# Core products of a triangle layer: two of three channels with one half-width product less, plain channels row block by row block, squares in PSUM banks that are tiles of their own

## The chip, the core and the metric

The kernel runs on one core of one Trainium2 chip. The metric is the device time of one execution in microseconds (us), as the median of several runs. A core has these engines: TensorE for matrix products (PE in the profile, with its weight loads as PEld), VectorE (DVE), ScalarE (ACT), GpSimd (POOL) and SyncE (SP), which here issues nearly all DMAs. Each engine works through its own queue in order, and semaphores make one wait for another. TensorE writes its results into PSUM, eight banks of 512 float32 numbers per partition; VectorE and ScalarE read and write PSUM and SBUF[...].

## The reference, cut to what matters

Two layers act on x of shape 1 x 384 x 384 x 128, in float32. The part that the change touches is the einsum of the first layer and the layer norm over channels that follows it.

```python
z = layernorm(x)
left  = (z @ Wl + bl) * sigmoid(z @ Wlg + blg)        # [i, k, h]
right = (z @ Wr + br) * sigmoid(z @ Wrg + brg)        # [j, k, h]
core  = einsum('bikh,bjkh->bijh', left, right)        # 128 channels h, each a 384x384x384 product
zo = layernorm(core, over h) @ Wout + bout
x1 = x + sigmoid(x @ Wg + bg) * zo
# second layer, row by row: left' = x1 @ (Wleft + Weq), right' summed over the row,
# out = (left' * rowsum * sigmoid(x1 @ Wgate)) @ Wout1;  result = layernorm(out + x1)
```

For one channel h the core is a product of two 384 x 384 matrices, that is of 3 x 3 blocks of 128 on the left side against 384 columns on the right. The layer norm over h needs, for each (i, j), the sum and the sum of squares of the core over all channels.

## The kernel before, in words

There are three stages. Stage 1 (to about 1012 us) normalises x, computes left and right and stores them to DRAM in `lr_d`, channel by channel; the last two row groups are kept in SBUF (`kept`). Stage 2 (about 1012 to 1737 us) computes the core, one channel after the other, and stores it to `core_d`. Stage 3 does the rest, row by row. Nearly every instruction goes through `seq`, so each engine's queue has the order in which the Python code issues it.

Stage 2, in which the change lies, has a loop over the channels h = 0 to 125; the last two, 126 and 127, follow in other code. With `NB = 3`, `N = 384`, `P = 128` and `J = 192`:

- `load_h` (L92) loads a channel's left and right parts, interleaved, from `lr_d` into a tile `lrh`, in two DMAs: 384 KB (the block k = 0) and 640 KB (k = 1 and most of k = 2). There are three such tiles. Each pass of the loop issues the load of h + 3 at its end, when channel h's tile is free.
- `stay` (L610, POOL) copies the kept rows of channel h + 1 into its tile, in block k = 2. `fill` (L585 to L592, POOL) does the like and the cast for the channels 0 and 127.
- `apart` (L632, ACT) casts the right part, which is interleaved in `lrh`, to a contiguous tile `rr`, one block k at a time; k = 0 needs the first DMA, k = 1 the second, k = 2 that and `stay`.
- A plain channel (before: even h) takes nine full-width products (128 x 128 against 384 columns), into one PSUM tile `pc` of three banks, for k outer and row block i inner. ACT copies the tile to SBUF as `ct` (L689) one channel later.
- A split channel (before: odd h) saves products by a scheme with sums of blocks in the manner of Strassen and Winograd: three full-width products for row block 2 (into bank `b4`), and eleven products of half width (192 columns) for the row blocks 0 and 1, into the banks `b0` to `b3`. Of the left side it needs four sums `ss` (`left_sums`, L618, POOL), of the right side four sums `tt` (`right_sums2`, L623 to L628, POOL); these are prepared one channel ahead, in the order stay, left sums, right sums. VectorE adds the partial results (`add`, L651): four adds to form terms, and four to write `ct`. ACT copies `b0` (L692) and `b4` (L696).
- `store_core` (L645, SP) stores `ct` (576 KB). `add_sum` (L638, VectorE) adds a channel to `csum`; `squares` (L635, ACT) squares `ct` into SBUF (`sq`), and `add_squares` (L642, VectorE) adds that to `csq`. Each is one instruction of 1152 columns.

Two engines that read the same PSUM tile do so one after the other, in program order. The three banks of `pc` are one tile; `b0` to `b4` are one each. SBUF sums and terms lie in one tile, `arena`, of eight rows of 384 columns.

Of the kernel before, what the change touches and what calls it, by code (L numbers as in the profile page):

```python
# [8 lines left out]
F32 = mybir.dt.float32  # L9
AF = mybir.ActivationFunctionType  # L10
# [4 lines left out]
P = 128  # L15
# [4 lines left out]
def triangle_then_gated_row_kernel(ctx: ExitStack, tc: tile.TileContext, a: dict, out: bass.AP):  # L20
# [13 lines left out]
    nc = tc.nc  # L34
    x_nat, x_tok, x_row = a["x_nat"], a["x_tok"], a["x_row"]
    NG8, C = x_nat.shape[1], x_tok.shape[2]
    N = 8 * NG8
    H = a["L0_side_b"].shape[0] // 4
    assert C == P and H == P and N % P == 0
    NB = N // P  # L40
# [15 lines left out]
    def seq(ins):  # L56

        return tc.keep_in_program_order(ins)
# [21 lines left out]
    with ExitStack() as ctx2:  # L80
# [16 lines left out]
        with tc.tile_pool(name="p1w", bufs=5, side="right") as wp, \  # L97
# [47 lines left out]
            wst, g0, b0 = stage[:, 0:4 * H], stage[:, 4 * H:4 * H + 1], stage[:, 4 * H + 1:4 * H + 2]  # L145
            brow, m1, d = stage[:, 5 * H:9 * H], stage[:, 9 * H:10 * H], stage[:, 10 * H:10 * H + 1]
# [16 lines left out]
            wz = const([P, 4 * H], "wz")  # L163
# [281 lines left out]
            for n in range(PLAIN, len(chunks)):  # L445
                k = 2 + (n - PLAIN) // 2
# [74 lines left out]
        arena = spool.tile([P, 2 + 2 * NB, N], F32, name="arena")  # L521
# [39 lines left out]

        with tc.tile_pool(name="p2r", bufs=2, side="right", reuse_waits="tile") as rrp, \
             tc.tile_pool(name="p2more", bufs=1, side="right", reuse_waits="tile") as more, \
             tc.tile_pool(name="p2out", bufs=3, side="right", reuse_waits="tile") as op, \
             tc.tile_pool(name="p2st", bufs=1, side="right", reuse_waits="tile") as stp:
            csum = spool.tile([P, NB, N], F32, name="csum")
            csq = spool.tile([P, NB, N], F32, name="csq")
            seq(nc.vector.memset(csum, 0.0))
# [4 lines left out]
            right = {}  # L573
# [21 lines left out]

            J = N // 2
            js = slice(0, J), slice(J, N)
            one, base, more2, least = (arena[:, n, j] for n in (2, 2 * NB) for j in js)
            tt = arena[:, 0:2].rearrange("p b n -> p (b n)").rearrange("p (q j) -> p q j", j=J)
            ss = [arena[:, 2 * NB + 1, n * P:(n + 1) * P] for n in range(3)] + [stp.tile([P, P], F32, name="s4")]  # L600
            sq = arena[:, NB:2 * NB]
            cts = {}

            def block(h, k, i):
                return loaded2[h][:, k, i * P:(i + 1) * P, 0]
# [5 lines left out]

            def left_sums(h):

                for n, x, y, op in ((0, block(h, 0, 1), block(h, 0, 0), ALU.subtract),
                                    (1, block(h, 0, 1), block(h, 1, 1), ALU.add),
                                    (2, ss[1], block(h, 0, 0), ALU.subtract),
                                    (3, block(h, 1, 0), ss[2], ALU.subtract)):
                    seq(nc.gpsimd.tensor_tensor(ss[n], x, y, op))  # L618

            def right_sums2(h):  # L620

                rr = right[h]
                seq(nc.gpsimd.tensor_tensor(  # L623
                    tt[:, 0:2], rr[:, 0, js[1]].unsqueeze(1).to_broadcast([P, 2, J]),
                    rr.rearrange("p b n -> p (b n)").rearrange("p (a m) -> p a m", a=2)[:, :, js[0]], ALU.subtract,
                ))
                seq(nc.gpsimd.tensor_tensor(tt[:, 2], rr[:, 0, js[0]], tt[:, 1], ALU.subtract))
                seq(nc.gpsimd.tensor_tensor(tt[:, 3], rr[:, 1, js[0]], tt[:, 2], ALU.subtract))  # L628

            def apart(h, k):  # L630

                seq(nc.scalar.copy(right[h][:, k], loaded2[h][:, k, :, 1]))  # L632

            def squares(h):
                seq(nc.scalar.activation(sq, cts[h], AF.Square))  # L635

            def add_sum(h, c=None):
                seq(nc.vector.tensor_add(csum, c or cts[h], csum))  # L638

            def add_squares(h):  # L640
                if h >= 0:
                    seq(nc.vector.tensor_add(csq, csq, sq))  # L642

            def store_core(h, queue=nc.sync):
                seq(queue.dma_start(out=core_d[:, h, :].rearrange("(b p) j -> p b j", p=P), in_=cts[h]))  # L645

            def product(to, lhsT, rhs, start=True, stop=True):
                seq(nc.tensor.matmul(to, lhsT=lhsT, rhs=rhs, start=start, stop=stop))  # L648

            def add(out, ps, term):  # L650
                seq(nc.vector.tensor_add(out, ps, term))  # L651

            def plain(h, banks):

                for k in range(NB):
                    for i in range(NB):
                        product(banks[i], block(h, k, i), right[h][:, k], k == 0, k == NB - 1)

            fill(0)
            with tc.tile_pool(name="p2mix", bufs=1, space=PSUM, reuse_waits="tile") as mps:  # L660
                pc = mps.tile([P, NB, 512], F32, name="pc")
                b0, b1, b2, b3 = (mps.tile([P, 512], F32, name="b%d" % n)[:, :J] for n in range(4))
                b4 = mps.tile([P, 512], F32, name="b4")[:, :N]
                for h in range(H - 2):
                    cts[h] = op.tile([P, NB, N], F32, tag="ct", name="ct")
                    right[h + 1] = rrp.tile([P, NB, N], F32, tag="rr", name="rr")
                    if h % 2 == 0:
                        plain(h, [pc[:, i, :N] for i in range(NB)])
                        if h > 0:
                            store_core(h - 1)  # L670
                        add_squares(h - 2)
                        stay(h + 1)
                        left_sums(h + 1)
                        for k in range(NB - 1):
                            apart(h + 1, k)
                        right_sums2(h + 1)
                        if h > 0:
                            squares(h - 1)
                            add_sum(h - 1)
                        apart(h + 1, NB - 1)  # L680
                        if h > 0:
                            add_squares(h - 1)
                    else:
                        rr, ct = right[h], cts[h]
                        B = [[rr[:, k, j] for j in js] for k in range(NB)]
                        product(b0, block(h, 0, 0), B[0][0])
                        for k in range(NB):
                            product(b4, block(h, k, 2), rr[:, k], k == 0, k == NB - 1)
                        seq(nc.scalar.copy(cts[h - 1], pc[:, :, :N]))  # L689
                        store_core(h - 1)  # L690
                        add_sum(h - 1, pc[:, :, :N])
                        seq(nc.scalar.copy(one, b0))  # L692
                        stay(h + 1)
                        for k in range(NB - 1):
                            apart(h + 1, k)
                        seq(nc.scalar.copy(ct[:, 2], b4))  # L696
                        apart(h + 1, NB - 1)
                        squares(h - 1)
                        product(b1, ss[2], tt[:, 2])
                        product(b2, ss[0], tt[:, 1])  # L700
                        product(b3, ss[1], tt[:, 0])
                        add(base, b1, one)
                        add(more2, b2, base)
                        add(base, b3, base)
                        add(least, b2, base)
                        product(b0, block(h, 1, 0), B[1][0], True, False)
                        product(b0, block(h, 2, 0), B[2][0], False, True)
                        product(b1, ss[3], B[1][1], True, False)
                        product(b1, block(h, 2, 0), B[2][1], False, True)
                        product(b3, block(h, 1, 1), tt[:, 3], True, False)  # L710
                        product(b3, block(h, 2, 1), B[2][0], False, True)
                        product(b2, block(h, 2, 1), B[2][1])
                        add(ct[:, 0, js[0]], b0, one)
                        add(ct[:, 0, js[1]], b1, base)
                        add(ct[:, 1, js[0]], b3, more2)
                        add(ct[:, 1, js[1]], b2, least)
                    del right[h], loaded2[h]
                    load_h(h + 3)
                store_core(h)
            with tc.tile_pool(name="p2ps", bufs=2, space=PSUM, reuse_waits="tile") as ps, \  # L720
                 tc.tile_pool(name="p2one", bufs=1, space=PSUM, reuse_waits="tile") as ps1:
                for h in range(H - 2, H):
# [11 lines left out]
                            start=(kb == 0), stop=(kb == NB - 1),  # L734
                        ))
                    if h == H - 2:
                        add_squares(h - 2)
                        squares(h - 1)
                        add_sum(h - 1)
                        add_squares(h - 1)  # L740
                        fill(h + 1)
                    ct = op.tile([P, NB, N], F32, tag="ct", name="ct")
                    to = core_d[:, h, :].rearrange("(b p) j -> p b j", p=P)
# [362 lines left out]
```

## Time and profile before

| | us |
|---|---|
| median of 3 runs (3136.75 to 3138.16) | 3137.22 |
| profiled execution, its own time | 3139.36 |
| span of the profiled execution | 3137.6 |
| stage 2, first product of channel 0 to first product of channel 126 | 1012.37 to 1725.93 |
| PE busy in the span | 3117.4 |
| DVE busy in the span | 2581.1 |
| POOL busy in the span | 2369.4 |
| ACT busy in the span | 1949.7 |

A row of the profile names the line of the kernel, the engine, the operation, the tile written and the tiles read, the shape, and the count; then the busy time, or in the timeline start and length. In brackets or after a bar stands for how long the engine was idle before and what released it. A float32 product shows as two records (two passes) of PE and of PEld. In the view of waits the columns are the total, the number of times and the longest. POOL's spans are rough.

### The profile page before, as it was taken

Reading aid. Unit: us, or ns where it says so; the run is one execution under the profiler, and the core shown is the slowest. Engines: PE = TensorE matmul, PEld = TensorE weight load, DVE = VectorE, ACT = ScalarE, POOL = GpSimd, SP = SyncE. Lnnn points to the kernel's source line nnn. Section 1 sums busy time; section 2 is a strip of 40 time slices with the busy share of each in tenths; the row PEclk is TensorE's granted clock in tenths of the full one; section 3 lists DMA queues with packets and bytes.
Section 4 is the critical chain, followed back from the end, with each engine's and each line's share of the span. In section 5 each row is a group of like instructions: output and inputs, shape, how many; then the busy total and the mean of one; then the engine's idle time right before and its main releaser. Section 6 shows DMA issues by size and latency. Waiting matters only on the chain.

```text
span 3137.6 us, 47186 instructions
## 1 busy us (share of the span) xinstructions
PE 3117.4 (99%) x11936; PEld 2209.1 (70%) x11936; DVE 2581.1 (82%) x7913; ACT 1949.7 (62%) x4196; POOL 2369.4 (76%) x3003
## 2 busy tenths in 40 slices
PE   9999999999999999999999999999999999999998
PEld 4677777777777777777777666777777777777776
DVE  8888888888886777777776888888888888888998
ACT  4444444444444666656666577777777777777776
POOL 6888888888886565666566588787887887888887
PEclk9999999999999999999999999999999999999999
DMA  4888978788883999999999866666666666666562
GB/s 153 327 312 293 334 276 332 287 321 311 292 333 89 288 289 291 291 290 290 290 290 290 296 213 221 217 222 222 222 222 222 220 223 215 222 218 222 205 216 105
DMA packets 509119, 797.61 MB, mean 254 GB/s; under 512 B 56689, under 2 KB 419569, under 8 KB 492466
## 3 DMA queue, kind: packets, MB, share of 16 engines
q1 hardware_dynamic: 507952, 793.20, 74.5%
q8 instruction: 100, 1.64, 0.2%
q14 instruction: 169, 1.38, 0.1%
q10 hardware_dynamic: 834, 1.18, 0.1%
q0 software_dynamic: 64, 0.20, 0.0%
HBM read 508.14 MB, written 286.36 MB: 253 GB/s over the span
## 4 chain that ended last, share of the span: by engine, by line
PE 98%; DVE 1%; ACT 0%; POOL 0%; issue 0%; DMA 0%; SPq 0%; POOLq 0%; DVEq 0%; ACTq 0%
PE pr L372 31%; PE pc L648 12%; PE b L648 11%; PE py L904 8%; PE pr L875 8%; PE pg L892 8%; PE pl L893 8%; PE pg L844 8%; PE py L905 4%; PE pc L732 0%; DMA stage<-in_x_nat_dram 0%; PE pq L852 0%; PE pt L335 0%; POOL rs L286 0%; DVE lr L385 0%
## 5 line engine op out<-in xcount | busy, mean ns | idle before, releaser
L372 PE MATMUL pr<-wz,xc 128*128 128x512 f32 x2176 | 935.2, 592 | 1.4 <-POOL xc L324 1.4
L372 PEld LDWEIGHTS pr<-wz,xc 128*128 128x128 f32 x2176 | 670.5, 308 | 265.4 <-POOL xc L324 2.7
L383 ACT ACTIVATE sg<-pr,rs 128x256 f32<-128x256 f32 x1152 | 482.8, 470 | 510.8 <-ACT sg L383 355.5
L385 DVE SCALAR_TENSOR_TENSOR lr<-pr,rs,sg 128x256 f32<-128x256 f32 x1152 | 501.9, 477 | 165.6 <-ACT sg L383 160.1
L939 ACT ACTIVATE py<-py,nm,rs 128x128 f32<-128x128 f32 x1149 | 491.9, 429 | 158.5 <-DVE u L897 80.0
L904 PEld LDWEIGHTS py<-wo,u 128*128 128x128 f32 x2304 | 376.6, 191 | 97.5
L904 PE MATMUL py<-wo,u 128*128 128x128 f32 x2304 | 402.0, 275 | 0.0
L866 POOL TENSOR_TENSOR cs<-ct,rt 128x384 f32<-128x384 f32 x380 | 378.7, 998 | 9.5 <-PE pr L875 4.1
L974 POOL TENSOR_TENSOR yt<-yt,lnb 128x384 f32<-128x384 f32 x380 | 379.8, 1001 | 2.9 <-DVE yt L968 2.5
L648 PE MATMUL pc<-rr,lrh 128*128 128x384 f32 x1134 | 376.1, 486 | 0.4 <-DVE lr L385 0.4
L324 POOL TENSOR_TENSOR xc<-xc,bc 128x512 f32<-128x512 f32 x272 | 345.6, 1270 | 24.0
L286 POOL TENSOR_TENSOR rs<-nd,mhalf 128x8 f32<-128x8 f32 (+1 forms) x145 | 236.2, 1629 | 147.0 <-ACT sg L383 107.4
L919 DVE BATCH_NORM_STATS2 st<-py 128x6 f32<-128x128 f32 x1152 | 266.1, 286 | 88.6 <-PE py L905 86.7
L905 PE MATMUL py<-ident,x1T 128*128 128x128 f32 x1152 | 314.0, 273 | 0.0
L875 PE MATMUL pr<-cs,wc 128*128 128x384 f32 x768 | 313.5, 490 | 0.0
L892 PE MATMUL pg<-x1T,mat_L_conv_W_gate 128*128 128x384 f32 x768 | 310.7, 486 | 0.9 <-ACT g L895 0.9
L632 ACT COPY rr<-lrh 128x384 f32<-128x384 f32 x378 | 205.0, 553 | 171.5 <-DMA lrh<-lr_d 108.4
L844 PE MATMUL pg<-xt,mat_L_conv_Wg 128*128 128x384 f32 x768 | 310.7, 487 | 0.3 <-ACT ct L758 0.2
L648 PEld LDWEIGHTS pc<-rr,lrh 128*128 128x128 f32 x1134 | 220.3, 196 | 128.4 <-issue 1.1
L893 PE MATMUL pl<-x1T,mat_L_conv_W_left 128*128 128x384 f32 x768 | 310.5, 486 | 0.0
L618 POOL TENSOR_TENSOR arena<-lrh 128x128 f32<-128x128 f32 x126 | 105.4, 837 | 259.4 <-DMA lrh<-lr_d 206.4
L895 ACT ACTIVATE g<-pg,col_L_conv_b_gate 128x384 f32<-128x384 f32 x384 | 222.7, 580 | 104.4 <-PE pg L892 93.9
(151 smaller groups left out, 5278.9 us busy)
## 6 DMA issues: line engine op xcount, KB each, us to landing
lr_d<-lr SPq DMA_DIRECT2D x128, 1024.0 KB
lrh<-lr_d SPq DMA_DIRECT2D x128, 640.0 KB
xt<-in_x_row_dram SPq DMA_DIRECT2D x96, 768.0 KB
ct<-core_d SPq DMA_DIRECT2D x95, 768.0 KB
rt<-rstd_d SPq DMA_DIRECT2D x95, 768.0 KB
core_d<-ct SPq DMA_DIRECT2D x126, 576.0 KB
out_dram<-yt SPq DMA_DIRECT2D x94, 768.0 KB
xt<-in_x_nat_dram SPq DMA_DIRECT2D x136, 512.0 KB
```

The source lines that it names most:

```text
L372: seq(nc.tensor.matmul(pr[:, r, :], lhsT=columns[n][:, 4 * q + i, :] if n < PLAIN else columns[n][:, q, :, i], rhs=wz, start=True, stop=Tr ...
L383: seq(nc.scalar.activation(sg[r], pr[:, r, 2 * H:], AF.Sigmoid, scale=rs[r]))
L385: seq(nc.vector.scalar_tensor_tensor(t[:, :, c * XR + r0 + r, :], pr[:, r, :2 * H].rearrange("k (h s) -> k h s", s=2), rs[r], sg[r].rearra ...
L648: seq(nc.tensor.matmul(to, lhsT=lhsT, rhs=rhs, start=start, stop=stop))
L844: seq(nc.tensor.matmul(pg[:, :N], lhsT=wg0, rhs=r["xT"], start=True, stop=True))
L875: seq(nc.tensor.matmul(pr[:, :N], lhsT=wc, rhs=r["cs"], start=True, stop=True))
L892: seq(nc.tensor.matmul(pg2[:, :N], lhsT=wgate, rhs=r["x1T"], start=True, stop=True))
L893: seq(nc.tensor.matmul(pl[:, :N], lhsT=wleft, rhs=r["x1T"], start=True, stop=True))
L904: seq(nc.tensor.matmul(py[:, s], lhsT=r["u"][:, s], rhs=r["wo"], start=True, stop=False))
L905: seq(nc.tensor.matmul(py[:, s], lhsT=r["x1T"][:, s], rhs=ident, start=False, stop=True, is_transpose=True))
L939: seq(nc.scalar.activation(py[:, s], py[:, s], AF.Identity, bias=bias, scale=scale))
L974: seq(engine.tensor_tensor(yt, yt, lnbb, ALU.add))
```

## The change

1. The channels go in threes (`kind = h % 3`): kind 0 is plain, kinds 1 and 2 are split. Before, they went in twos. Of the 126 channels, 42 are plain and 84 split; before, 63 and 63.
2. A plain channel goes row block by row block (i outer, k inner), into three one-bank tiles `full3` (named `r0` to `r2`) in place of `pc`. ACT copies each to `ct`, and VectorE adds each to `csum`, by itself.
3. Squares are written into PSUM: those of the plain channel in place in `full3` (in the kind 1 channel), those of the first split channel into `full3` (in the kind 2 channel), those of the second into the banks of `b0` to `b2` (in the plain channel). All are 384 columns wide, and VectorE adds them from there to `csq`.
4. Of `tt` and `ss` there are two sets, one for each kind of split channel: the second `tt` where the squares lay in `arena`, the second `ss` in `wz`, the weights of stage 1. `left_sums` and `right_sums2` for the second split channel are issued in the first one. The pool `p2st` goes.
5. The last four adds of a split channel are parted: `join` (row block 0) and `close` (row block 1, then the store and `add_sum`). For kind 1, `join` stands at the end of its own channel and `close` at the start of the next; for kind 2 both stand in the following plain channel. The banks `b2` and `b3` have changed parts, and the terms lie in `terms2`.

```diff
-            one, base, more2, least = (arena[:, n, j] for n in (2, 2 * NB) for j in js)
-            tt = arena[:, 0:2].rearrange("p b n -> p (b n)").rearrange("p (q j) -> p q j", j=J)
-            ss = [arena[:, 2 * NB + 1, n * P:(n + 1) * P] for n in range(3)] + [stp.tile([P, P], F32, name="s4")]
+            terms2 = arena[:, 2:4].rearrange("p b n -> p (b n)").rearrange("p (q j) -> p q j", j=J)
+            base = arena[:, 6, js[0]]
+            tts = [arena[:, n:n + 2].rearrange("p b n -> p (b n)").rearrange("p (q j) -> p q j", j=J) for n in (0, 4)]
+            sss = [[arena[:, 2 * NB + 1, n * P:(n + 1) * P] for n in range(3)] + [arena[:, 6, J:J + P]],
+                   [wz[:, n * P:(n + 1) * P] for n in range(4)]]
...
-            def squares(h):
-                seq(nc.scalar.activation(sq, cts[h], AF.Square))
...
+            def squares(c, out):
+                seq(nc.scalar.activation(out, c, AF.Square))
+
+            def add_squares(c, ib=slice(0, NB)):
+                seq(nc.vector.tensor_add(csq[:, ib], c, csq[:, ib]))
+
+            def add_sum(c, ib=slice(0, NB)):
+                seq(nc.vector.tensor_add(csum[:, ib], c, csum[:, ib]))
...
-                pc = mps.tile([P, NB, 512], F32, name="pc")
-                b0, b1, b2, b3 = (mps.tile([P, 512], F32, name="b%d" % n)[:, :J] for n in range(4))
+                full3 = [mps.tile([P, 512], F32, name="r%d" % n)[:, :N] for n in range(NB)]
+                half4 = [mps.tile([P, 512], F32, name="b%d" % n) for n in range(4)]
                 b4 = mps.tile([P, 512], F32, name="b4")[:, :N]
+                b0, b1, b2, b3 = (b[:, :J] for b in half4)
+
+                def join(h):
+                    for b, j, n in (b0, js[0], 0), (b1, js[1], 1):
+                        add(cts[h][:, 0, j], b, terms2[:, n])
+
+                def close(h):
+                    for b, j, n in (b2, js[0], 2), (b3, js[1], 3):
+                        add(cts[h][:, 1, j], b, terms2[:, n])
+                    store_core(h)
+                    add_sum(cts[h])
...
-                    if h % 2 == 0:
-                        plain(h, [pc[:, i, :N] for i in range(NB)])
+                    kind, rr, ct = h % 3, right[h], cts[h]
+                    if kind == 0:
+                        for i in range(NB):
+                            for k in range(NB):
+                                product(full3[i], block(h, k, i), rr[:, k], k == 0, k == NB - 1)
                         if h > 0:
-                            store_core(h - 1)
-                        add_squares(h - 2)
+                            join(h - 1)
+                            close(h - 1)
                         stay(h + 1)
                         left_sums(h + 1)
                         for k in range(NB - 1):
                             apart(h + 1, k)
                         right_sums2(h + 1)
+                        seq(nc.scalar.copy(ct[:, 0], full3[0]))
                         if h > 0:
-                            squares(h - 1)
-                            add_sum(h - 1)
+                            for ib in range(NB):
+                                squares(cts[h - 1][:, ib], half4[ib][:, :N])
+                                add_squares(half4[ib][:, :N], ib)
                         apart(h + 1, NB - 1)
-                        if h > 0:
-                            add_squares(h - 1)
+                        seq(nc.scalar.copy(ct[:, 1], full3[1]))
+                        for ib in range(2):
+                            add_sum(full3[ib], ib)
                     else:
...
                         product(b0, block(h, 0, 0), B[0][0])
                         for k in range(NB):
                             product(b4, block(h, k, 2), rr[:, k], k == 0, k == NB - 1)
-                        seq(nc.scalar.copy(cts[h - 1], pc[:, :, :N]))
-                        store_core(h - 1)
-                        add_sum(h - 1, pc[:, :, :N])
-                        seq(nc.scalar.copy(one, b0))
                         stay(h + 1)
-                        for k in range(NB - 1):
-                            apart(h + 1, k)
-                        seq(nc.scalar.copy(ct[:, 2], b4))
+                        if kind == 1:
+                            seq(nc.scalar.copy(cts[h - 1][:, 2], full3[2]))
+                            store_core(h - 1)
+                            add_sum(full3[2], 2)
+                            seq(nc.scalar.copy(terms2[:, 0], b0))
+                            left_sums(h + 1)
+                            for ib in range(2):
+                                squares(full3[ib], full3[ib])
+                                add_squares(full3[ib], ib)
+                            for k in range(NB - 1):
+                                apart(h + 1, k)
+                            right_sums2(h + 1)
+                            seq(nc.scalar.copy(ct[:, 2], b4))
+                            squares(full3[2], full3[2])
+                        else:
+                            close(h - 1)
+                            seq(nc.scalar.copy(terms2[:, 0], b0))
+                            for ib in 0, 2:
+                                squares(cts[h - 1][:, ib], full3[ib])
+                            apart(h + 1, 0)
+                            squares(cts[h - 1][:, 1], full3[1])
+                            apart(h + 1, 1)
+                            add_squares(full3[0], 0)
+                            seq(nc.scalar.copy(ct[:, 2], b4))
                         apart(h + 1, NB - 1)
-                        squares(h - 1)
                         product(b1, ss[2], tt[:, 2])
-                        product(b2, ss[0], tt[:, 1])
-                        product(b3, ss[1], tt[:, 0])
-                        add(base, b1, one)
-                        add(more2, b2, base)
-                        add(base, b3, base)
-                        add(least, b2, base)
+                        product(b2, ss[1], tt[:, 0])
+                        product(b3, ss[0], tt[:, 1])
+                        add(base, b1, terms2[:, 0])
+                        add(terms2[:, 2], b3, base)
+                        add(terms2[:, 1], b2, base)
+                        add(terms2[:, 3], b3, terms2[:, 1])
...
-                        product(b3, block(h, 1, 1), tt[:, 3], True, False)
-                        product(b3, block(h, 2, 1), B[2][0], False, True)
-                        product(b2, block(h, 2, 1), B[2][1])
-                        add(ct[:, 0, js[0]], b0, one)
-                        add(ct[:, 0, js[1]], b1, base)
-                        add(ct[:, 1, js[0]], b3, more2)
-                        add(ct[:, 1, js[1]], b2, least)
+                        product(b2, block(h, 1, 1), tt[:, 3], True, False)
+                        product(b2, block(h, 2, 1), B[2][0], False, True)
+                        product(b3, block(h, 2, 1), B[2][1])
+                        if kind == 1:
+                            add_squares(full3[2], 2)
+                            join(h)
+                        else:
+                            for ib in 1, 2:
+                                add_squares(full3[ib], ib)
                     del right[h], loaded2[h]
                     load_h(h + 3)
-                store_core(h)
+                join(h)
+                close(h)
```

More of the change, by code (lines that the diff above doesn't have):

```diff
@@ L563, in triangle_then_gated_row_kernel @@
              tc.tile_pool(name="p2more", bufs=1, side="right", reuse_waits="tile") as more, \
-             tc.tile_pool(name="p2out", bufs=3, side="right", reuse_waits="tile") as op, \
-             tc.tile_pool(name="p2st", bufs=1, side="right", reuse_waits="tile") as stp:
+             tc.tile_pool(name="p2out", bufs=3, side="right", reuse_waits="tile") as op:
             csum = spool.tile([P, NB, N], F32, name="csum")
@@ L612, in left_sums @@
             def left_sums(h):
+                ss = sss[h % 3 - 1]
                 for n, x, y, op in ((0, block(h, 0, 1), block(h, 0, 0), ALU.subtract),
@@ L620, in right_sums2 @@
             def right_sums2(h):
-                rr = right[h]
+                rr, tt = right[h], tts[h % 3 - 1]
                 seq(nc.gpsimd.tensor_tensor(
@@ L632, in apart @@
                 seq(nc.scalar.copy(right[h][:, k], loaded2[h][:, k, :, 1]))
-            def squares(h):
-                seq(nc.scalar.activation(sq, cts[h], AF.Square))
[L637 to L642, printed above, removed]
+            def squares(c, out):
[4 more added lines that the diff above has]
+                seq(nc.vector.tensor_add(csum[:, ib], c, csum[:, ib]))
             def store_core(h, queue=nc.sync):
@@ L651, in add @@
                 seq(nc.vector.tensor_add(out, ps, term))
[L653 to L657, printed above, removed]
             fill(0)
             with tc.tile_pool(name="p2mix", bufs=1, space=PSUM, reuse_waits="tile") as mps:
-                pc = mps.tile([P, NB, 512], F32, name="pc")
-                b0, b1, b2, b3 = (mps.tile([P, 512], F32, name="b%d" % n)[:, :J] for n in range(4))
+                full3 = [mps.tile([P, 512], F32, name="r%d" % n)[:, :N] for n in range(NB)]
+                half4 = [mps.tile([P, 512], F32, name="b%d" % n) for n in range(4)]
                 b4 = mps.tile([P, 512], F32, name="b4")[:, :N]
+                b0, b1, b2, b3 = (b[:, :J] for b in half4)
[7 more added lines that the diff above has]
+                    add_sum(cts[h])
                 for h in range(H - 2):
@@ L676, in triangle_then_gated_row_kernel @@
                         right_sums2(h + 1)
+                        seq(nc.scalar.copy(ct[:, 0], full3[0]))
                         if h > 0:
-                            squares(h - 1)
-                            add_sum(h - 1)
+                            for ib in range(NB):
+                                squares(cts[h - 1][:, ib], half4[ib][:, :N])
+                                add_squares(half4[ib][:, :N], ib)
                         apart(h + 1, NB - 1)
-                        if h > 0:
-                            add_squares(h - 1)
+                        seq(nc.scalar.copy(ct[:, 1], full3[1]))
+                        for ib in range(2):
+                            add_sum(full3[ib], ib)
                     else:
-                        rr, ct = right[h], cts[h]
+                        ss, tt = sss[kind - 1], tts[kind - 1]
                         B = [[rr[:, k, j] for j in js] for k in range(NB)]
@@ L736, in triangle_then_gated_row_kernel @@
                     if h == H - 2:
[L737 to L740, printed above, removed]
+                        squares(cts[h - 1], sq)
+                        add_squares(sq)
                         fill(h + 1)
```

## The prediction

> **What bounds the kernel now.** I read the page first, then the chain of work that ended last, then, for the stage of the core products (about 1012 to 1726 us), the table of windows, the waits, the instructions by tile, and the timeline of a few channels. Of the page, the engines' shares and the chain's; of the chain in order of time, four pieces (start, length, what); of the windows, one of 120 us (busy time of PE, PEld, DVE, ACT, POOL, then granted clock, DMA share, GB/s):
>
> ```profile
> PE 3117.4 (99%) x11936; PEld 2209.1 (70%) x11936; DVE 2581.1 (82%) x7913; ACT 1949.7 (62%) x4196; POOL 2369.4 (76%) x3003
> PE 98%; DVE 1%; ACT 0%; POOL 0%; issue 0%; DMA 0%; SPq 0%; POOLq 0%; DVEq 0%; ACTq 0%
> ...
> 1012.37 6.05 PE pc L648 x18
> 1018.42 5.51 PE b L648 x28
> 1023.93 5.80 PE pc L648 x18
> 1029.73 5.51 PE b L648 x28
> ...
> 1320.00:1440.00 120.00, 120.00 (x485) 87.02 (x484) 84.88 (x124) 72.91 (x118) 75.43 (x119) 1.00 0.97 290
> ```
>
> TensorE is the chain. In the stage it is busy 120.00 of 120.00 us at a granted clock of 1.00, and the chain alternates a plain channel (18 passes, 5.80 us) with a split one (28 passes, 5.51). A product is two passes: 5.805/9 = 0.645 for full width, (5.51 - 3 x 0.645)/11 = 0.325 for half width. A split channel thus costs 0.295 less than a plain one. VectorE has 85 of 120 us and the DMA share is 0.97: these two could become the bound. So the waits (longest in the last column), a group of POOL's ops by tile (min/median/max ns), two DMA windows and the timeline:
>
> ```profile
> POOL arena L618 <- DMA lrh<-lr_d: 174.7, 81, 3.7
> DVE csum L638 <- ACT ct L689: 99.6, 54, 2.5
> ACT rr L632 <- DMA lrh<-lr_d: 91.1, 76, 2.5
> PEld b L648 <- POOL arena L627: 0.4, 2, 0.2
> ...
> L618 POOL TENSOR_TENSOR s<-lrh,arena x53: 459/1452/1668, 1107.7 to 1697.2; 128x128 f32<-128x128 f32 x53
> ...
> 1404.00:1405.60 1.60, 1.60 (x6) 0.97 (x5) 0.83 (x1) 1.60 (x4) 1.44 (x4) 1.00 0.70 210
> 1405.60:1410.00 4.40, 4.40 (x25) 3.94 (x24) 3.72 (x10) 2.80 (x5) 1.40 (x5) 1.00 1.05 313
> ...
> 1408.93 5.97 PE L648 MATMUL pc<-rr,lrh 128*128 128x384 f32 x18
> 1409.41 1.35 DVE L642 TENSOR_TENSOR csq<-csq,arena 128x1152 f32<-128x1152 f32 x1
> ...
> 1410.67 1.67 DVE L638 TENSOR_TENSOR csum<-ct,csum 128x1152 f32<-128x1152 f32 x1
> 1411.53 0.56 ACT L632 COPY rr<-lrh 128x384 f32<-128x384 f32 x1 [1.53 <-DMA lrh<-lr_d]
> ...
> 1417.59 1.67 DVE L651 TENSOR_TENSOR arena<-b,arena 128x192 f32<-128x192 f32 x4
> ```
>
> Others wait for DMA, for TensorE or for each other; TensorE waits for nobody but 0.4 us in all. The second half of a channel's load lands 2.6 us into the plain channel before it (1411.53 - 1408.93); over the stage the trace's completion records put it at 1.5 to 3.2 after the start-up, median about 2. It falls back to 1.5 within a channel or two after every late one, so the queue drains. The DMA engines move 313 GB/s when full and dip to 210 once per channel.
>
> **TensorE, the path.** The products go from 1449 to 1554 (42 x 9 + 84 x 14), half-width ones from 693 to 924. From the second channel on, before: 1018.25 to 1725.93 = 707.7 us (62 plain and 63 split make 707.0; 0.6 is waits). After: 84 x 5.51 + 41 x 5.805 = 700.9 without waits. That is -6.8.
>
> **The first channel, +0.65.** Row block by row block, the third product (k = 2) is due 1.3 us into a channel instead of 3.9. In channel 0 its right side is completed by POOL's copy of the last kept rows, which follows the last op of the stage before: in the timeline it runs 1014.07 to 1014.31. From there 7 of 9 products are still to do: 1014.37 + 7 x 0.645 = 1018.9, against 1018.25. It cannot be nothing (order and copy are both fixed); without any loss -0.3 (r0 and r1 need not wait for the last reader, as pc did, 0.37), with a slow restart +0.9. In later plain channels ACT's cast of k = 2 ends at L + 1.5 of the channel before (L: when its load's second half has landed), due 6.5: some 3 us ahead.
>
> **VectorE, beside it.** Per three channels: 16 adds of 192 columns, 12 of 384, 2 of 1152; 30 instead of 18 ops. 0.357 for 192 and 1.357 for 1152 (PSUM source) give 0.56 for 384; SBUF-only 1152 take 1.40. 16 x 0.357 + 12 x 0.56 + 2 x 1.40 = 15.2 of 16.8 us, 90%, from 75%. A rule speaks against this. First the rows: L638 starts 1.26 after L642, which took 1.35, so the next op starts before the last has ended. The Trainium skill (VectorE: DVE Perf Modes, The DRAIN you can't avoid) says that each op is followed by a drain of about its duration less 266 ns, though it grants that an op which isn't held starts earlier. Drained, the three channels would take 15.2 + 16 x 0.09 + 12 x 0.29 + 2 x 1.13 = 22.4 us, and the kernel would be 42 x 5.6 = 235 us slower; a pair of today would need 8 x 0.45 + 4 x 2.5 = 13.6 of its 11.3. The trace decides: 15.2.
>
> **Queues, walked through by durations.** Engines react 0.03 to 0.04 after a release; a product's result is readable 0.2 after its slot. ACT starts a 384-column op every 0.45; its work per three channels is some 12.4 of 16.8 us (27 ops), room enough, so only its order matters.
> - Plain channel (ACT 8 ops, VectorE 10): VectorE closes the former split channel (its b3 ends at 0.2) by about 1.1, stores it, adds it by 2.5, then waits for ACT's squares into b0 to b2. These stand behind the cast of the second load half (landing L): b0 is free for the next channel at L + 2.0, due 5.6, so L up to 3.6 is free.
> - First split channel: full3[2] is copied at 0.2, the store goes at 0.7 (now 1.3). The four adds keep today's times (first at 2.85, b3 at 3.43, last starts at 4.1), add_squares(full3[2]) at 4.39, join's b0 4.86 to 5.22. TensorE loads weights for the next channel's b0 at 5.35. Cover: 0.1 us, the thinnest anywhere. ACT's squares(full3[2]) ends at L + 1.4, so this holds up to L = 3.0.
> - Second split channel: close, store at 0.7, add_sum to 2.1, all before the adds at 2.85; TensorE's next need of a bank is loose by 0.4 or more.
> - POOL: 84 preparations instead of 63, and the second stands directly behind the first in the queue. Undisturbed it takes 4.1 us after L (0.5 + 0.46 x 2 + 0.99 + 0.59 x 2, and gaps); it is due 7.4 after the channel's start. L618 at 459 against a median 1452 shows that it is held, by about what an op of VectorE with two SBUF operands lasts; of these there are 3 x 1.4 us per pair now and 2 x 1.4 per three channels after, since squares are then read from PSUM. So POOL, with a third more of this work, still gets looser.
> - SP: the stores are issued 0.3 to 0.6 us earlier, each still behind the former load and ahead of the next; 126 stores and all loads stay. Loads still go at a channel's end, 0.3 earlier in one of six.
>
> Squares written into PSUM have no row of this shape: 0.48 (L696, PSUM to SBUF) below, 0.63 above (L939, in place, 0.43 at 128 columns, stretched by ACT's 0.8 ns per column). I take 0.5, the 384-column square at L753 being 0.53; even at 0.63 the thin spot holds to L = 2.8. Stationary tiles in wz instead of arena: the same 190 ns load. Full banks as tiles of their own let VectorE start at one bank instead of three; it isn't late, so this is worth nothing by itself. Leaving the stage: the first product of channel 126 waits for the last add_squares, 0 to 0.2.
>
> **Sum.** -6.8 + 0.65 = -6.2 at most. For waits I take 0.5: today's are 0.6, the thin spot opens for L over 3.0 in few channels, and POOL's are mostly gone. -5.7. The profiled execution took 3139.36 with a span of 3137.6, the median of the runs is 3137.22; a saving inside the span carries over: 3131.5.
>
> **Rivals.**
> - Slower, by late loads at the thin spot. In the first split channel squares(full3[2]) stands behind the cast of the landing half, add_squares behind it, join behind that, and the next channel's first product behind join. From L = 3.0 on each further us is paid by TensorE in full, 42 times. At L = 3.15 the gain is gone, at 3.3 (0.3 x 42 = 12.6) the kernel is 6.4 slower: 3143.6. For it: cover of only 0.1, a DMA share of 0.97, a period 0.05 shorter. Against it: median L about 2, drained after each late load.
> - The DMA becomes the bound. A channel moves 173.7 MB/106 = 1.64 MB; at 309 GB/s (mean of the full windows around 1404 to 1420) 5.3 us, and 5.61 are wanted. If today's 5.66 were its limit, only the first channel's loss would remain: 3137.9. The dips to 0.70 speak against it. A mild form, waits of 0.05 to 0.1 per three channels, gives 3133.5 to 3136.
> - The split doesn't bring 0.295: against it, both channel lengths are in the chain and the products are counted.
>
> **Chances.** About 0.2% (6.3 us) is what a measurement of this kernel can tell from no change; my largest gain of 6.2 lies just inside. The forecast 0.75 (3131.0 to 3132.8, of which 0.17 may come out over 0.2% if no wait is left or the start loses less), DMA or small waits 0.16, slower 0.09. Faster 0.17, same 0.74, slower 0.09. The range reaches from no waits and a cheaper start, 3130.4, over the mild DMA case to 3136.4.
>
> **What would show it.** In the profile after: chain still 98% PE; channels of 5.80, 5.51, 5.51; a gap of about 1 us on TensorE near 1013 released by POOL's copy; DVE at 85 to 90% in the stage; POOL's 128x128 ops mostly near 0.5; stage end near 1719.7 to 1720.5. I am wrong if PE shows waits for DVE at the b0 product of every third channel, if ACT's wait for DMA falls well over 3 us into a channel, or if VectorE's start-to-start times are longer than its durations.

## The result, and the profile after

The changed kernel takes 3131.15 us (median of 20 runs, 3129.96 to 3134.5) against 3137.58 of the kernel before in the same session (20 runs): 6.4 us less, a ratio of 0.998 with a 95% interval of 0.9973 to 0.9987. A second session gave 3131.21 against 3137.31 (0.9981, 0.9974 to 0.9988). The forecast was 3131.5, in a range of 3130.4 to 3136.4. The profiled execution is one of the longer ones, 3133.74 us with a span of 3131.9; what it lost is found in the last section.

From the page, the engines and the chain that ended last; then the chain in order of time at the start of stage 2 (start, length, what); then the window of 120 us that was shown of before:

```profile
PE 3111.3 (99%) x12146; PEld 2234.8 (71%) x12146; DVE 2640.4 (84%) x8415; ACT 1957.8 (63%) x4551; POOL 2387.5 (76%) x3150
PE 98%; DVE 1%; issue 0%; POOL 0%; ACT 0%; DMA 0%; POOLq 0%; ACTq 0%; DVEq 0%; SPq 0%
...
1013.14 0.24 POOL lrh L584
1013.38 0.18 POOL rr L585
1013.57 0.04 issue
1013.61 4.79 PE r L649 x14
1018.40 11.02 PE b L649 x56
1029.42 5.80 PE r L649 x18
1035.23 11.02 PE b L649 x56
...
1320.00:1440.00 120.00, 120.00 (x527) 92.62 (x526) 96.39 (x215) 74.92 (x180) 78.06 (x146) 1.00 0.99 294
```

TensorE has less to do (3111.3 us busy instead of 3117.4) and is still 98% of the chain. Two split channels of 5.51 now follow a plain one of 5.80. The start of the chain shows the price: before the 14 passes that were left of channel 0 the chain runs over POOL's two copies. VectorE works 96 of 120 us instead of 85, and the DMA share has gone from 0.97 to 0.99, from 290 to 294 GB/s.

The view of waits for 1100 to 1700 us (total, times, longest) has no line in which PE or PEld waits for anybody; its first lines, and POOL's sums by tile (min/median/max ns):

```profile
POOL arena L620 <- DMA lrh<-lr_d: 170.3, 70, 5.6
ACT rr L634 <- DMA lrh<-lr_d: 79.4, 59, 2.7
ACT arena L719 <- PE b L649: 73.6, 36, 2.3
DVE arena L652 <- PE b L649: 47.2, 142, 0.4
...
L620 POOL TENSOR_TENSOR arena<-lrh,arena x36: 459/462/466, 1099.9 to 1688.8; 128x128 f32<-128x128 f32 x36
L620 POOL TENSOR_TENSOR wz<-lrh,wz x36: 459/462/468, 1105.4 to 1694.0; 128x128 f32<-128x128 f32 x36
L611 POOL COPY lrh<-lr x216: 282/291/1495, 1102.7 to 1697.4; 128x128 f32<-128x128 f32 x108
```

The last left sum took 459/1452/1668 before, and each of its 27 long ones in 1100 to 1700 us ended 0.32 us after an op of VectorE with two SBUF operands. It is held no more in either set. What of these ops is left (`csum<-ct`) now holds copies of `stay` instead: 30 of 216 take up to 1.5 us, and each of them ends 0.15 us after such an op. TensorE doesn't wait for them.

### The profile page after: what moved, and what is told of

The parts are those of the page before. It is cut to its first block, busy times and chain, and to the rows that moved or that the text cites. A ratio compares the mean times of both kernels' runs of the same rounds, so it can differ in the third digit from the quotient of the medians.

```text
span 3131.9 us, 48235 instructions
## 1 busy us (share of the span) xinstructions
PE 3111.3 (99%) x12146; PEld 2234.8 (71%) x12146; DVE 2640.4 (84%) x8415; ACT 1957.8 (63%) x4551; POOL 2387.5 (76%) x3150
## 4 chain that ended last, share of the span: by engine, by line
PE 98%; DVE 1%; issue 0%; POOL 0%; ACT 0%; DMA 0%; POOLq 0%; ACTq 0%; DVEq 0%; SPq 0%
PE pr L372 31%; PE b L649 15%; PE py L934 8%; PE pr L905 8%; PE pg L922 8%; PE pl L923 8%; PE r L649 8%; PE pg L874 8%; PE py L935 4%; DMA core_d<-ct 0%; PE pc L764 0%; POOL rs L286 0%; PE pq L882 0%; PE pt L335 0%; DVE lr L385 0%
## 5 line engine op out<-in xcount | busy, mean ns | idle before, releaser
L649 PE MATMUL b<-rr,lrh 128*128 128x192 f32 (+1 forms) x1512 | 374.4, 379 | 0.0
L649 PEld LDWEIGHTS b<-rr,lrh 128*128 128x128 f32 x1512 | 268.4, 196 | 53.0
L876 ACT ACTIVATE gT<-pg,col_L_conv_bg 128x384 f32<-128x384 f32 x384 | 220.4, 576 | 105.0 <-PE pg L874 105.0
```

## The experiments

Each kernel was timed in five rounds with the kernel before on the same chip. "Stage" below is the stretch from the first product of channel 1 to that of channel 126, read from TensorE's records: 707.68 us before, 700.84 after.

### e1_again: the changed kernel once more

> The changed kernel once more, as the measure for the other runs of this chip. Both theories (TensorE's issue sets the stage; the load or VectorE's queue sets it) give the time of the first measurement, 3131.2 within 0.6. Its trace tells whether the 1.6 us that TensorE lost at the start of stage 3 in the first profile (waiting for the core load) come back: if they are part of the change, again 1.4 to 1.8; if they are chance, some other value.

3131.21 us (17 runs). Stage 700.84 again. TensorE's wait at the start of stage 3 didn't return, so it is no part of the change.

### e2_start: k = 2 last in channel 0

```diff
-                        for i in range(NB):
-                            for k in range(NB):
-                                product(full3[i], block(h, k, i), rr[:, k], k == 0, k == NB - 1)
+                        todo = [(i, k) for i in range(NB) for k in range(NB)]
+                        if h == 0:
+                            todo.sort(key=lambda o: o[1] == NB - 1)
+                        for i, k in todo:
+                            product(full3[i], block(h, k, i), rr[:, k], k == 0, k == NB - 1)
```

> Channel 0 alone takes its products with k = 2 last (all row blocks), the other plain channels stay row block by row block. If the loss at the start is the wait of the third product for POOL's copy (1.24 us of gap and 0.11 of restart in the trace of the changed kernel), it goes: 1.3 us faster than the changed kernel, 3129.8. If the gap only takes up slack that the next channels have anyway, nothing: 3131.2.

3129.27 us (8 runs), 1.9 less than e1_again. The chain at the start of stage 2:

```profile
1003.83 5.58 PE pr L372 x13
1009.41 5.80 PE r L649 x18
1015.22 11.02 PE b L649 x56
```

The way over POOL is gone, and channel 0 takes the 5.80 us of any plain channel. From TensorE's last pass in stage 1 to channel 126 it is 707.08 us instead of 708.44 (in e1_again): 1.36 less, what the gap of 1.24 and its restart were. The other 0.6 lies outside this stretch, and I put it down to scatter between runs. So the loss at the start was real, and it could be avoided.

### e3_pairs: the other parts without the 21 split channels

```diff
-                    kind, rr, ct = h % 3, right[h], cts[h]
+                    kind, rr, ct = h % 2, right[h], cts[h]
...
-                ss = sss[h % 3 - 1]
+                ss = sss[0]
...
-                            join(h - 1)
                             close(h - 1)
```

(`tts[0]` likewise; the sums for a second split channel go.)

> One part alone: channels in twos as before (63 plain, 63 split), with the new plain order, squares in PSUM and the parted adds. If the gain is the 21 channels that take 0.295 less, all of it is gone and the start's loss stays: stage 707.0 from channel 1 on, 3137.6 - 0.6 (today's waits of the kernel before) + 0.65 = 3137.6 within 0.8. If squares in PSUM and less blocking of POOL bring something by themselves, it is faster than the kernel before by over 2 us. POOL's 128x128 ops fall from a mean of 0.86 to about 0.52 us in either case.

3137.37 us (13 runs) against 3137.31 of the kernel before: ratio 1.0, 0.9992 to 1.0009. Stage 707.45, against 707.04 for 62 x 5.805 + 63 x 5.51; the 0.41 between them is a single wait, shown below. Its window, and two groups of POOL:

```profile
1320.00:1440.00 120.00, 120.00 (x492) 88.11 (x491) 88.63 (x194) 76.75 (x183) 54.77 (x119) 1.00 0.97 290
...
L620 POOL TENSOR_TENSOR arena<-lrh x106: 513/519/913, 1100.6 to 1692.2; 128x128 f32<-128x128 f32 x106
L620 POOL TENSOR_TENSOR arena<-lrh,arena x53: 460/463/468, 1104.3 to 1693.3; 128x128 f32<-128x128 f32 x53
```

With squares in PSUM the same work keeps POOL busy for 55 instead of 75 of 120 us, and this brings no time: POOL was not on the path. The gain is the number of products; the other parts bring nothing by themselves. Squares in SBUF with channels in threes was not tried: the second `tt` lies where those squares lay.

The single wait shows what a late load does. The second half of a load landed 4.11 us into the plain channel that began at 1451.91, later than the 3.6 up to which the prediction had called it free. The cast waited for it, the square into b0 stood behind the cast, VectorE's add behind the square, and TensorE's next product into b0 behind the add:

```profile
1456.04 0.55 ACT L634 COPY rr<-lrh 128x384 f32<-128x384 f32 x1 [1.49 <-DMA lrh<-lr_d]
1456.86 1.32 ACT L637 ACTIVATE b<-ct 128x384 f32<-128x384 f32 x3
1457.40 1.49 DVE L640 TENSOR_TENSOR csq<-b,csq 128x384 f32<-128x384 f32 x3 [3.28 <-ACT b L637]
1458.01 1.93 PEld L649 LDWEIGHTS b<-rr,lrh 128*128 128x128 f32 x8 [0.74 <-DVE csq L640]
```

### e4_kouter: plain channels with k outer again

```diff
-                        for i in range(NB):
-                            for k in range(NB):
+                        for k in range(NB):
+                            for i in range(NB):
                                 product(full3[i], block(h, k, i), rr[:, k], k == 0, k == NB - 1)
```

> Undo one part: all plain channels with k outer and row block inner, all else as in the changed kernel. By the walk of the queues ACT's copy of r0 waits until 4.7 us into the plain channel instead of 2.1, the squares into b0 start at 5.15 and VectorE has read them at about 6.2, where TensorE loads weights for b0 at 5.65: a wait of 0.55 to 0.65 in each of 42 groups, 23 to 27 us, less 1.3 at the start: 3153 to 3157, with TensorE's waits at the b0 product after each plain channel, released by VectorE. If ACT and VectorE are slack enough and the order doesn't matter: 3129.9.

3152.07 us (5 runs): 20.9 more than e1_again, just under the 3153 to 3157 expected, and slower than the kernel before by a ratio of 1.0047 (1.0035 to 1.006). Two lines of its waits from 1100 to 1700 us, and the timeline of one plain channel, begun at 1409.33:

```profile
PEld b L649 <- DVE csq L640: 30.7, 35, 0.9
PE b L649 <- DVE csq L640: 9.4, 35, 0.3
...
1414.05 0.48 ACT L687 COPY ct<-r 128x384 f32<-128x384 f32 x1 [1.22 <-PE r L649]
1414.42 1.32 ACT L637 ACTIVATE b<-ct 128x384 f32<-128x384 f32 x3
1414.96 1.49 DVE L640 TENSOR_TENSOR csq<-b,csq 128x384 f32<-128x384 f32 x3 [3.03 <-ACT b L637]
1415.57 1.93 PEld L649 LDWEIGHTS b<-rr,lrh 128*128 128x128 f32 x8 [0.88 <-DVE csq L640]
```

ACT's copy of r0 waits for a product 4.7 us into the channel, the square into b0 stands behind it, VectorE's add behind that, and TensorE's next product into b0 behind that. The stage is 723.18 us: 22.3 more, in 41 waits of 0.54; channel 0, with k = 2 last, gives back 1.35. I had 0.55 to 0.65 in 42 groups; ACT's square followed the copy after 0.37 instead of 0.45, and the group of channel 0 has no squares. Row block by row block is what lets squares go into `b0` to `b2` without a wait of TensorE.

### e5_later_join: one more VectorE op ahead of join

```diff
                             add_squares(full3[2], 2)
+                            add(full3[1], full3[2], csq[:, 2])
                             join(h)
```

> The changed kernel with one more VectorE op of 384 columns (into a PSUM bank that is free then; the outputs are the same) ahead of join in the first split channel. In the trace of the changed kernel join's b0 ends 0.17 us before TensorE loads weights for the next channel's b0, in all 42 groups. If that cover is real and nothing else stands behind it, the op shifts join by about 0.48 and TensorE waits 0.2 to 0.3 in each of 42 groups: 8 to 13 us slower than the changed kernel, 3139 to 3144, and the whole gain is gone. If TensorE has other slack there: within 1 of 3131.2.

3149.46 us (5 runs): 18.3 more than e1_again, over the 8 to 13 expected. First the timeline of the changed kernel at the end of a first split channel, then the chain of this experiment:

```profile
1409.58 0.55 DVE L640 TENSOR_TENSOR csq<-r,csq 128x384 f32<-128x384 f32 x1
...
1410.05 1.24 DVE L652 TENSOR_TENSOR ct<-b,arena 128x192 f32<-128x192 f32 x4
1410.07 3.07 PE L649 MATMUL b<-rr,lrh 128*128 128x192 f32 x12
```

```profile
1310.53 5.51 PE b L649 x28
1316.04 0.20 issue
1316.23 5.76 PE b L649 x28
```

In the changed kernel join's first add runs 1410.05 to 1410.39, and the weights for the next channel's b0 are loaded at 1410.56: 0.17 of cover, in all 42 groups within 0.002. The extra op reads the row of `csq` that was just written and started only when add_squares had ended, 0.58 after its start and not 0.48, and join moved by 0.60. TensorE lost 0.445 per group (0.60 - 0.17, and 0.02): the stage is 18.7 longer. Once the cover is used up, the rest is paid in full. The view of the chain calls a part of it "issue", which here hides a wait of TensorE's own queue for VectorE's semaphore: the record of that wait ends 0.045 after join's first add.

### e6_join_first: more cover

```diff
-                            add_squares(full3[2], 2)
                             join(h)
+                            add_squares(full3[2], 2)
```

(on top of e2_start)

> Channel 0 with k = 2 last, as in e2_start, and in the first split channel join ahead of add_squares. If the thin spot costs nothing today (cover 0.17 in every group), only its cover grows by about 0.48, and the time is that of e2_start, 3129.3 within 0.6. If late loads now and then open it: faster than e2_start by up to 1.5.

3129.42 us (12 runs). Stage 700.84, as in e2_start. The cover grew from 0.17 to 0.63, and nothing came of it, since it had never been used up.

### e7_less: how near the DMA is

```diff
-                        product(b2, block(h, 1, 1), tt[:, 3], True, False)
-                        product(b2, block(h, 2, 1), B[2][0], False, True)
+                        product(b2, block(h, 1, 1), tt[:, 3])
```

(on top of e6_join_first)

> As e6_join_first, but each split channel leaves out one half-width product (block (2, 1) with the first half of the right side, so that part of the core is left out). If TensorE's issue alone sets the stage, 84 x 0.325 = 27.3 us faster than e6_join_first, about 3102, with the DMA share at its top: 1.64 MB in 5.39 us are 304 GB/s, just under my estimate of 309. If the DMA is the bound already (share 0.99), nearly nothing: 3127 to 3129. In between, the load waits tell how near it is: ACT and POOL waits for DMA that reach TensorE.

3103.13 us (4 runs), 26.3 less than e6_join_first. Stage 674.32, 26.5 less. Its chain and its window:

```profile
1301.37 5.80 PE r L649 x18
1307.17 10.37 PE b L649 x52
...
1320.00:1440.00 120.00, 120.00 (x518) 91.36 (x517) 98.56 (x221) 79.92 (x191) 82.21 (x153) 1.00 1.02 305
```

Two split channels take 10.37 instead of 11.02, TensorE is busy throughout, and the DMA engines carry 305 GB/s. So neither they at 294 nor VectorE at 80% are the bound of the changed kernel. Of the 27.3 to be had 0.8 is missing, 0.6 of it in four waits of 0.06 to 0.30: three behind loads that landed 3.76, 3.77 and 4.04 us into a plain channel, one at the end of the stage.

### e8_more_dma: 56 KB more in each channel

```diff
                     load_h(h + 3)
+                    seq(nc.sync.dma_start(out=extra[h % 2], in_=lr_d[0, :, h, :112]))
```

(on top of e2_start)

> As e2_start, with one more DMA of 56 KB in each channel behind the load, into a tile that nobody reads: 3.5% more traffic, 302 GB/s at the same pace. If TensorE sets the pace, the time of e2_start, 3129.3, up to 3 more for single late loads. If the DMA does at its present 292 GB/s, 0.035 x 5.61 x 126 = 25 us more: 3154.

3130.14 us (11 runs), 0.9 more than e2_start. The window of the same stretch:

```profile
1320.00:1440.00 120.00, 120.00 (x530) 93.00 (x530) 96.26 (x214) 75.33 (x181) 76.80 (x144) 1.00 1.02 303
```

Stage 700.84, to the hundredth: 3.5% more traffic costs nothing there. The 0.9 lies outside the stage, and within the scatter of runs.

## Why the prediction was right, point by point

- **TensorE, the path.** 84 x 5.51 + 41 x 5.805 = 700.9 was said for the stage, 700.84 is measured; before 707.68. This step, -6.8, carries the result, and e3_pairs shows it by its absence: no additional split channels, no gain.
- **The first channel.** +0.65 was said. From the last pass of stage 1 to the first product of channel 1 it is 6.85 before and 7.58 after, so +0.74: the wait for POOL's copy that was named (1.24, and 0.11 of slower restart), less about 0.6, since channel 0 begins 0.43 after that pass instead of 0.97 and no longer restarts slowly there (0.08). e2_start takes the wait away.
- **Waits.** 0.5 was allowed, none came. Whether the late loads reach TensorE hangs on L, when the second half of a load lands. After the change it was at most 3.2 us into a plain channel (limit said: 3.6), 2.9 into a first split one (3.0) and 3.4 into a second one; medians 2.3, 2.0 and 2.0. The limits were near, and no load passed them. The limit in the plain channel was well placed: in e7_less a load at 3.69 cost nothing, those at 3.74 to 3.77 cost 0.03 to 0.06, one at 4.04 cost 0.33, and the one at 4.11 in e3_pairs 0.41. So it lies near 3.7, and beyond it TensorE pays nearly in full. The sum without waits, -6.8 + 0.74 = -6.1, is what the two sessions show with 6.4 and 6.1.
- **What can be told.** The prediction held 6.3 us for the least that a measurement can tell from no change. The interval of 0.9973 to 0.9987 is narrower than that: it leaves no change out, and the stage lengths show the gain without scatter.
- **The thin spot.** Named in the right place, with a cover of 0.1; measured 0.17. e5_later_join shows that what goes beyond the cover is paid, and e6_join_first that the spot cost nothing in the changed kernel.
- **VectorE.** Mis-sized: 15.2 of 16.8 us was the sum of durations, and ops that overlap were counted twice; busy is 96.4 of 120, thus 13.5 of 16.8. The rows' verdict against the drain held: in the line of four `ct` adds above, 0.35 each, they take 1.24 together, so the next starts before the last has ended. ACT has 25 ops per three channels, not 27. Neither moved the forecast.
- **POOL.** Looser, as said: with a third more of this work it is busy 78 of 120 us instead of 75.
- **The rivals.** The DMA as the bound falls by e7_less and e8_more_dma. The slower case by late loads did not come. That a late load reaches TensorE is shown, but at the product after a plain channel. At the thin spot of the first split channel, where the rival had it, no run shows it: in the changed kernel no load came later than 2.9 there, and in e8_more_dma one at 3.1 still brought no wait.

A better version came out: e2_start (3129.27, ratio to before 0.9976, 0.9966 to 0.9986) and with it e6_join_first (3129.42, 0.9976, 0.9968 to 0.9985).

## What to carry to other kernels

When one engine is busy without a gap, count its work in its own units and walk the other queues through one period with start-to-start times: the gain is the count, provided that each release on that engine keeps some cover. Write down that cover per place, since a cover of 0.17 us costs nothing, and a shift of 0.60 cost 0.445 in every round. Look apart at the first round: an order that is free in the steady state can wait for the last work of the stage before.

## What the runs showed that I had not expected

The stage is the same to 0.01 us in every run with the same order, while what lies around it is not. The last pass of stage 1, which no kernel changed, began between 1008.8 and 1011.4 us in the ten profiles. In three of them TensorE lost time early in stage 3. In the first profile of the changed kernel it waited for VectorE, which waited for the first load of the core:

```profile
1740.64 1.48 DVE L894 TENSOR_TENSOR cs<-ct,pb 128x384 f32<-128x384 f32 x3 [3.77 <-DMA ct<-core_d]
...
1741.24 0.91 PE L905 MATMUL pr<-cs,wc 128*128 128x384 f32 x2 [1.42 <-DVE cs L894]
```

It lost 1.58 there. e8_more_dma lost 0.59 at the same product, behind a wait of VectorE that the view puts down to POOL, and e6_join_first 0.55 some 9 us later, behind an op of POOL; the other seven lost nothing. Why these come late now and then stays open. So a difference of 1 or 2 us between two single spans says little, where one between two stage lengths says much.

And the DMA share of 0.97 was no warning: at 305 GB/s in e7_less it reads 1.02 with four short waits of TensorE, and in e8_more_dma, where it reads 1.02 too, TensorE didn't wait at all in the stage.
